# Two hand-made instruction orders replaced, and slabs issued by halves, in a two-layer banded convolution kernel

## The chip, the cores and the metric

The kernel runs on one core of one Trainium2 chip. The metric is the device time of one execution in microseconds (us), as the median of the runs. All arithmetic is in 32-bit floating point; nearly all of it is done by small matmuls on TensorE (PE), with VectorE (DVE), ScalarE (ACT) and GpSimd (POOL) around them, and SyncE (SP) issuing the transfers.

## What is computed

The input x has 512 x 512 positions of 64 channels. Two layers of the same form follow each other, each `x = x + conv(_gn(x))`, where `_gn` normalises groups of two channels over the whole image. The core of one layer, from the reference (the masks are ones, the biases zeros):

```
xn = _ln(x, norm_scale, norm_bias)                       # over the 64 channels
left  = (xn @ Wl + bl) * sigmoid(xn @ Wlg + blg)         # 64 -> 128 channels
right = (xn @ Wr + br) * sigmoid(xn @ Wrg + brg)
out_gate = sigmoid(xn @ Wog + bog)
# _banded_ingoing, w = 4: out[:, i, j] = sum over d = -4..4 of left[:, i+d, i] * right[:, i+d, j]
out = _ln(_banded_ingoing(left, right, 4), out_norm_scale, out_norm_bias) * out_gate
return out @ Wo + bo                                     # 128 -> 64 channels
```

The left part is only needed in the nine diagonals of the band; the right part, the gate and the output are needed at every position.

## The kernel before

**Tiling.** The 512 rows are cut into 9 blocks of 64 rows that step by 56, each block's columns into 4 chunks, and each chunk into 8 units. A layer therefore has 36 chunks and 288 units. The left parts that a block needs lie in SBUF as the tile `A`: 8 slabs, each loaded by two DMAs of 256 KB from `left_of`, one for each half of the partitions. A slab may only be overwritten when the last band of the block that uses it is done.

**Steps.** A unit passes through named steps, each a function `on_...` in `layer`: `load` (two DMAs into `z`), `scale` and `move` (POOL: the group norm), `inner` (DVE: statistics), `centre` and `resc` (POOL), `ztr` (PE: transposes), `keep0/1` (ACT: `ZT`, `zT`), `proj0/1` (PE), `sig0/1` (ACT: `sg`), `right0/1` (DVE: `RO<-banks,sg`). When the eight units of a chunk are there, eight `band` steps (PE: `banks<-RO,A`) and eight `copy` steps (`RO<-banks`) follow. Then, unit by unit: `ost` (DVE: statistics), `gate` (PE: `banks<-ZT,pack`), `gated` (ACT: `ZH<-banks`), `norm0` to `norm7` (ACT or POOL: `on<-RO`), `turn0/1` (PE: `banks<-ident,on`), `tg` (DVE: `ZH<-banks,pack,ZH`), `last` (PE: `bank<-pack,ZH`), `fetch` (two DMAs that load x into `XR`), `end` (DVE: `XR<-bank,XR`), `stp` (two DMAs that store). In layer 1 `sums` (PE: `acc<-XR`) adds up what layer 2's group norm needs; in layer 2 `seed` (PE) starts the output's accumulation. Every four units `sa` (ACT) and `sd0` to `sd13` (DVE) work out the inverse roots (`rs`, `nm`) for the two layer norms.

**What sets the order.** Two tables of words, `FIRST` for layer 1 and `SECOND` for layer 2, are walked once in each period, for `period in range(-4, n_chunks + 5)`. The word `sig1:-13` issues step `sig1` for unit `-13 + 8 * period`. A `!` moves a `norm` from ACT to POOL, a `copy` from ACT to DVE, and a number behind `@` asks for a PSUM bank. The helper `InOrder` (line 504, which is why nearly all rows of the profile carry L504) keeps the order of the program on each engine, so a table is the queue of all five engines; an instruction whose input is late holds up all that stand behind it on its engine.

**Banks.** Three double banks of PSUM (tiles named `banks`) are handed out by `take` and returned by `give`; `ztr`, `proj`, `band`, `gate` and `turn` each take one. PE then waits for the instruction (ACT or DVE) that last read this bank. The sums of layer 1 and the scratch of the inverse roots share one tile, `acc_bank`:

```
acc_bank = psa.tile([P, 512], F32, name="acc")
acc, work = acc_bank[:, : D + 1], [acc_bank[:, P:]]
```

The waits are set by tile, so in layer 1 PE's `sums` and DVE's `sd` steps wait for each other although they use different columns. Layer 2 has a `work` tile of its own and no sums.

**SP.** SP issues every transfer in program order. The semaphores of its DMAs are eight, used in turn, so a DMA also waits for the one eight before it. `slab` issues what stands next in the list `slabs`, to which `on_copy` adds a slab when its last band of a block is copied; where the list is empty the step does nothing, so slabs are loaded at every fourth period, when the row block changes.

Of the kernel before, what the change touches and what calls it, by code (L numbers as in the profile page):

```python
# [38 lines left out]
FIRST = """
end:-14 sd10:-12 inner:-6 sd11:-12 sd9:-12 turn1:-13 proj0:-14@0 proj1:-14@1 sd12:-12 tg:-13  # L40
sig0:-14 norm6:-12 sig1:-14 norm1:-12 resc:-12 resc:-11 norm3:-12! norm4:-12 right0:-14 right1:-14
last:-13 inner:-5 end:-13 inner:-8 band:-12@2 norm5:-12! norm2:-12 norm7:-12! norm0:-12! gate:-11@0
copy:-12 turn1:-12@1 turn0:-12 gated:-11 resc:-10 norm0:-11! ost1:-7 norm7:-11! norm4:-11!
proj1:-13@2 proj0:-13@0 tg:-12 stp:-17 centre:-8 norm2:-11! norm1:-11! centre:-9 load:-1 slab:-56
ost0:-5 sig1:-13 centre:-6 scale:-3 ost1:-5 ost3:-6 ztr:-12@1 norm3:-11 ost2:-7 sums:-16 sums:-15
sums:-17 right1:-13 ost3:-5 last:-12 ztr:-11@2 keep0:-12 keep1:-12 sig0:-13 norm5:-11 norm6:-11
turn0:-11@1 turn1:-11 norm1:-10! ost0:-6 ost3:-8 right0:-13 ost2:-8 end:-12 keep0:-11 keep1:-11
proj1:-12@0 load:0 fetch:-11 norm6:-10! norm0:-10! resc:-9 norm2:-10 scale:-4 tg:-11 proj0:-12@2
ost2:-5 sig1:-12 norm7:-10 right1:-12 ost0:-7 ost2:-6 ost0:-8 ost3:-7 ost1:-6 ost1:-8 gate:-10@1
sig0:-12 norm4:-10 ztr:-10@0 sums:-13 last:-11 norm3:-10 keep1:-10 keep0:-10 right0:-12 end:-11  # L50
gated:-10 sa:-8 sd0:-8 norm5:-10! move:-3 gate:-9@0 turn0:-10@2 gated:-9 norm5:-9! sd1:-8 turn1:-10
proj1:-11@1 tg:-10 sd2:-8 sd3:-8 ost0:-1 sd5:-8 sd4:-8 sig1:-11 load:1 load:2 stp:-12 slab:-112
stp:-14 slab:8 fetch:-10 stp:-13 right1:-11 proj0:-11@0 proj1:-10@2 sums:-14 last:-10 sd6:-8
sig0:-11 norm4:-9 sig1:-10 norm6:-9 norm0:-9! norm3:-9! scale:-1 norm7:-9! norm1:-9! norm2:-9!
right0:-11 ztr:-9@1 sd7:-8 sd8:-8 sd13:-8 right1:-10 turn0:-9@0 turn1:-9 proj0:-10@2 sd10:-8 sd9:-8
move:-4 resc:-8 keep0:-9 keep1:-9 tg:-9 proj1:-9@1 move:-1 resc:-6 sd11:-8 ost3:-4 sd12:-8
proj0:-9@0 sig0:-10 right0:-10 ztr:-8@2 sums:-12 end:-10 sig1:-9 norm1:-8 sig0:-9 right1:-9
right0:-9 last:-9 norm0:-8! scale:-2 norm2:-8 norm6:-8 keep1:-8 band:-6@1 gate:-8@0 load:3 stp:-11
fetch:-9 norm7:-8! norm4:-8! norm3:-8! norm5:-8 keep0:-8 ost0:-3 ost1:-1 turn0:-8@2 turn1:-8 scale:0
centre:-7 norm2:-7! norm6:-7! end:-9 ost2:-3 resc:-7 copy:-6 move:-2 gated:-8 norm5:-7! norm0:-7  # L60
norm7:-7 norm1:-7 gate:-7@1 ost3:-2 norm3:-7 band:-7@0 tg:-8 inner:-4 sums:-10 last:-8 stp:-10
fetch:-8 fetch:-7 scale:1 norm4:-7! gated:-7 copy:-7 ztr:-7@2 ost2:-2 ost0:-2 ost3:-1 ost3:-3
inner:-2 inner:-3 end:-8 gate:-6@1 centre:-5 keep1:-7 gated:-6 keep0:-7 ost1:-3 band:-5@0 copy:-5
turn1:-7@1 turn0:-7 move:1 ost0:-4 proj1:-8@2 proj0:-8@0 tg:-7 norm2:-6 norm0:-6 sig0:-8 ost2:-1
ost1:-4 ost1:-2 ost2:-4 sig1:-8 band:-1@1 norm4:-6! sums:-11 copy:-1 last:-7 move:0 norm3:-6!
resc:-5 norm5:-6! right1:-8 inner:-1 right0:-8 ztr:-6@2 norm6:-6 sa:-4 gate:-5@1 norm1:-6! norm7:-6!
load:4 centre:-3 keep0:-6 keep1:-6 end:-7 sd0:-4 gated:-5 sd1:-4 sd2:-4 slab:-96 band:-3@0 copy:-3
turn0:-6@2 scale:3 scale:2 norm0:-5! turn1:-6 norm6:-5! norm3:-5! proj0:-7@1 proj1:-7@0 sd3:-4
slab:-16 norm2:-5 fetch:-6 sig0:-7 norm1:-5 tg:-6 sd4:-4 sd5:-4 centre:-2 centre:-4 sig1:-7 norm7:-5
slab:40 load:6 fetch:-4 fetch:-5 sd6:-4 band:-8@2 right0:-7 gate:-4@1 sd7:-4 right1:-7 sd8:-4 move:2  # L70
ztr:-5@0 sd13:-4 last:-6 stp:-7 inner:1 copy:-8 norm4:-5 stp:-8 slab:48 slab:0 load:5 move:3
keep0:-5 keep1:-5 norm5:-5 gated:-4 band:-2@2 turn0:-5@0 copy:-2
"""


SECOND = """
gated:-1 slab:-72 load:11 fetch:-1 sd12:0 band:1@2 ost0:5 inner:4 stp:-4 fetch:3 slab:-48 fetch:0
norm5:0 norm3:0 norm0:0 scale:6 copy:1 norm1:0 norm6:0 resc:0 ost1:4 seed:-1 tg:-1 gate:1@0 fetch:1
ztr:0@1 last:-1 band:2@2 keep1:0 keep0:0 gated:1 ost3:7 ost1:7 inner:5 ost2:6 ost1:5 end:-1 resc:1
move:6 norm2:0! norm4:0! turn0:0@1 stp:-1 norm7:0! centre:3 turn1:0 copy:2 norm0:1! seed:0 proj0:0@0  # L80
norm4:1 tg:0 norm3:1! norm5:1! centre:4 scale:11 norm6:1! norm1:1! ztr:1@2 sig0:0 band:6@1 norm7:1
keep1:1 keep0:1 norm2:1 last:0 proj1:0@2 copy:6 ost2:7 inner:7 right0:0 ost1:6 inner:6 load:13
fetch:2 ost0:7 end:0 sa:4 turn1:1@0 turn0:1 seed:1 band:4@1 sd0:4 sig1:0 norm3:2 scale:10 norm2:2!
resc:2 sd1:4 tg:1 sd2:4 right1:0 proj0:1@0 norm4:2 norm6:2 copy:4 sd3:4 gate:2@2 band:5@1 resc:3
norm1:2! norm0:2! move:10 sig0:1 norm7:2 sd5:4 sd4:4 right0:1 move:11 norm5:2 gated:2 turn0:2@0
turn1:2 proj1:1@2 copy:5 scale:9 ztr:2@1 last:1 norm0:3! norm7:3 norm3:3 sig1:1 keep1:2 keep0:2
norm5:3 norm1:3 norm4:3 sd6:4 inner:10 sd7:4 sd8:4 sd13:4 tg:2 norm2:3! scale:13 norm6:3! centre:7
band:7@0 right1:1 end:1 sd10:4 sd11:4 gate:3@2 copy:7! turn1:3@1 turn0:3 sd12:4 gated:3 sd9:4 seed:2
ztr:3@0 last:2 band:3@2 inner:11 tg:3 end:2 keep0:3 norm1:4 move:9 resc:4 norm2:4 centre:5 norm4:4!
norm0:4! norm7:4! seed:3 norm5:4 norm6:4! keep1:3 slab:-16 proj0:2@1 inner:8 inner:9 copy:3 gate:4@0  # L90
centre:6 ost2:8 ost3:11 sig0:2 norm3:4 proj1:2@2 gated:4 load:12 stp:0 sig1:2 right0:2 turn0:4@1
turn1:4 stp:-2 ztr:4@0 slab:32 slab:-8 fetch:4 fetch:5 norm6:5! norm0:5! slab:32 load:16 stp:1
norm7:5 norm2:5! norm4:5! keep1:4 norm3:5 ost2:10 ost1:10 keep0:4 norm5:5! norm1:5 ost2:9 ost3:8
right1:2 last:3 gate:5@2 turn1:5@0 turn0:5 tg:4 resc:7 norm0:6! norm5:6! norm2:6! gated:5 proj0:3@1
end:3 ost1:11 proj1:3@2 norm6:6 sig0:3 resc:5 resc:6 scale:12 norm1:6! centre:8 centre:9 tg:5 sig1:3
norm7:6 norm4:6 seed:4 right0:3 ost0:9 right1:3 proj0:4@0 ost3:10 ost1:8 proj1:4@1 sig0:4 right0:4
sig1:4 norm3:6 ztr:5@2 right1:4 last:4 ztr:6@0 ost0:8 ost1:9 scale:16 slab:40 stp:3 load:15 keep0:5
centre:10 gate:6@1 end:4 keep1:5 ost0:10 ost2:11 ost3:9 keep1:6 keep0:6 gated:6 scale:15 proj0:5@2
turn0:6@0 turn1:6 seed:5 ost0:11 tg:6 proj1:5@1 last:5 ztr:7@0 norm3:7 sig0:5 move:15 ost2:12
fetch:6 sa:8 norm2:7! sig1:5 load:14 load:17 stp:2 slab:48 right0:5 sd0:8 right1:5 end:5 keep0:7  # L100
keep1:7 proj0:6@2 sd1:8 ost3:13 sd2:8 ost0:14 sig0:6 proj1:6@1 sd3:8 sig1:6 proj0:7@0 norm5:7
norm0:7 norm1:7! norm7:7! norm4:7! move:12 right0:6 seed:6 proj1:7@2 sd4:8 right1:6 gate:8@1 sd5:8
ost3:14 sd6:8 sig0:7 norm6:7 sig1:7 right0:7 stp:5 load:18 sd7:8 last:6 right1:7 sd8:8 band:8@0
ost0:12 gated:8 gate:7@2 sd13:8 ost3:12 sd10:8 end:6 sd9:8 move:16 sd11:8 ost2:13 turn1:7@1 turn0:7
move:13 copy:8
"""


# [1214 lines left out]
```

## Time and profile before

| | before |
|---|---|
| median of 3 runs (lowest to highest) | 4062.65 us (4057.47 to 4071.81) |
| profiled execution, its span | 4060.92 us, 4059.1 us |
| PE busy | 3652.7 us, 90% of the span |
| weight loads of PE (PEld) busy | 3167.1 us, 78% |
| DVE busy | 3592.6 us, 89% |
| ACT busy | 3222.3 us, 79% |
| POOL busy | 3562.2 us, 88% |
| granted clock, mean | 0.992 |
| DMA engines, mean busy | 50% by q1 (all of SP's transfers, 579.92 MB), 1.3% by q8 (instructions, 12.26 MB) |

The span is one run through the whole program. Its first 336.5 us are the statistics of the input, the weights and the filling of the pipeline of layer 1; from there to 2107.9 us layer 1 runs in periods of eight units, each with about 1378 PE instructions, and after the change of layers layer 2 does so from 2299.1 to 3993.1 us. In both of these stretches the granted clock is 1.00. Four engines are busy for 79 to 90% of the span, so the busy shares alone don't tell which one sets the time; the stretches of single periods do.

### The profile page before, as it was taken

Reading aid. Unit: us, or ns where it says so; the run is one execution under the profiler, and the core shown is the slowest. Engines: PE = TensorE matmul, PEld = TensorE weight load, DVE = VectorE, ACT = ScalarE, POOL = GpSimd, SP = SyncE. Lnnn points to the kernel's source line nnn. Section 1 sums busy time; section 2 is a strip of 40 time slices with the busy share of each in tenths; the row PEclk is TensorE's granted clock in tenths of the full one; section 3 lists DMA queues with packets and bytes.
Section 4 is the critical chain, followed back from the end, with each engine's and each line's share of the span. In section 5 each row is a group of like instructions: output and inputs, shape, how many; then the busy total and the mean of one; then the engine's idle time right before and its main releaser. Section 6 shows DMA issues by size and latency. Waiting matters only on the chain. (4 is left out here: it accounts for less than half of the span.)

```text
span 4059.1 us, 222567 instructions
## 1 busy us (share of the span) xinstructions
PE 3652.7 (90%) x94986; PEld 3167.1 (78%) x94986; DVE 3592.6 (89%) x9915; ACT 3222.3 (79%) x6120; POOL 3562.2 (88%) x4818
## 2 busy tenths in 40 slices
...
GB/s 397 334 130 95 155 117 154 120 160 116 157 119 154 116 146 123 147 128 151 133 100 120 128 155 128 154 132 158 130 160 122 159 126 157 127 160 124 165 111 103
DMA packets 562867, 595.72 MB, mean 147 GB/s; under 512 B 134742, under 2 KB 398966, under 8 KB 559572
## 3 DMA queue, kind: packets, MB, share of 16 engines
q1 hardware_dynamic: 559364, 579.92, 50.0%
q8 instruction: 748, 12.26, 1.3%
...
## 5 line engine op out<-in xcount | busy, mean ns | idle before, releaser
L504 POOL TENSOR_SCALAR on<-RO,rs,nm 128x128 f32<-128x128 f32 x2376 | 1050.4, 454 | 220.8 <-PE banks L504 174.7
L504 ACT ACTIVATE on<-RO,nm,rs 128x128 f32<-128x128 f32 x2232 | 1029.0, 500 | 24.0 <-PE banks L504 15.5
L504 PE MATMUL banks<-pack,ZT 64*128 64x128 f32 x9216 | 980.0, 282 | 35.0 <-DVE acc L504 14.9
L504 PE MATMUL banks<-pack,zT 64*128 64x128 f32 x9216 | 935.1, 273 | 0.6 <-issue 0.5
L504 ACT ACTIVATE sg<-banks 128x512 f32<-128x512 f32 x1170 | 691.7, 594 | 244.2 <-PE banks L504 215.9
L504 DVE BATCH_NORM_STATS2 sto<-RO 128x6 f32<-128x256 f32 x2304 | 859.6, 413 | 18.0 <-ACT RO L504 18.0
L504 DVE TENSOR_TENSOR RO<-banks,sg 128x512 f32<-128x512 f32 x1152 | 785.1, 683 | 93.8 <-ACT sg L504 74.9
L504 PEld LDWEIGHTS banks<-pack,ZT 64*128 64x128 f32 x9216 | 758.7, 189 | 82.2 <-PE banks L504 18.6
L504 DVE SCALAR_TENSOR_TENSOR ZH<-banks,pack,ZH 128x896 f32<-128x896 f32 (+1 forms) x576 | 667.6, 1159 | 134.4 <-PE banks L504 81.1
L504 PEld LDWEIGHTS banks<-RO,A 64*64 64x64 f32 x36864 | 614.2, 135 | 211.3 <-ACT ZH L504 45.4
L504 PE MATMUL banks<-RO,A 64*64 64x64 f32 x36864 | 698.5, 222 | 63.4 <-issue 26.2
L504 PEld LDWEIGHTS banks<-pack,zT 64*128 64x128 f32 x9216 | 746.9, 189 | 0.6 <-issue 0.6
L504 POOL TENSOR_TENSOR z<-z,rs 128x512 f32<-128x512 f32 x586 | 611.4, 1054 | 93.3 <-DVE rs L504 67.2
L504 PE MATMUL bank<-pack,ZH 128*64 128x64 f32 x18432 | 658.0, 224 | 25.1 <-DVE ZH L504 12.0
L504 POOL TENSOR_TENSOR z<-z,ga 128x512 f32<-128x512 f32 x556 | 649.9, 1172 | 32.4 <-DVE ga L425 18.0
L504 PEld LDWEIGHTS bank<-pack,ZH 128*64 128x64 f32 x18432 | 588.1, 138 | 85.0 <-issue 35.3
L504 POOL TENSOR_TENSOR z<-z,gb 128x512 f32<-128x512 f32 x556 | 645.2, 1171 | 3.1
L504 ACT COPY RO<-banks 128x1024 f32<-128x1024 f32 x540 | 547.0, 1013 | 106.2 <-PE banks L504 94.5
L504 POOL TENSOR_TENSOR z<-z,sti 128x512 f32<-128x512 f32 x586 | 621.3, 1069 | 5.5 <-DVE sti L504 5.5
L504 ACT ACTIVATE ZH<-banks 128x896 f32<-128x896 f32 (+1 forms) x576 | 535.5, 930 | 88.6 <-PE banks L504 45.7
L504 PE MATMUL banks<-ZT,pack 64*128 64x448 f32 (+1 forms) x2304 | 585.0, 575 | 2.0 <-issue 1.7
L504 DVE BATCH_NORM_STATS2 sti<-z 128x6 f32<-128x128 f32 x2344 | 506.6, 281 | 30.0 <-POOL z L504 29.6
...
## 6 DMA issues: line engine op xcount, KB each, us to landing
...
A<-left_of SPq DMA_DIRECT2D x288, 256.0 KB
...
```

The costliest lines, as they stand in the source:

```text
L504: return lambda *a, **k: tc.keep_in_program_order(f(*a, **k))
```

## The change

The two tables are replaced as a whole. No word of the new ones names a bank, and `take` hands out the bank that has been free longest, where it handed out the lowest-numbered free one. A `slab` word issues one half of a slab (one DMA) instead of both, and each new table has 16 such words instead of 8; the number and the sizes of the DMAs stay. In `FIRST` three of 35 `norm` steps per period go from POOL to ACT; in `SECOND` 31 of them stay on POOL, and the one `copy` on DVE goes to ACT. The lag between a unit's `proj` and its `end` stays at two periods, the tables' first and last words move by some units. All else that is computed, and every instruction of PE, is the same.

```diff
 FIRST = """
...
-stp:-14 slab:8 fetch:-10 stp:-13 right1:-11 proj0:-11@0 proj1:-10@2 sums:-14 last:-10 sd6:-8
...
+ost0:9 ost1:8 norm0:5 sums:0 sums:2 sig1:3 ost3:10 ost2:9 ost3:8
...
+norm2:5! norm3:5! sums:-1 sums:1 ost2:11 ost0:11 right1:3 last:4 slab:0
...
 SECOND = """
...
     def take(b: str) -> tuple:
 
         free = [n for n in range(3) if given[n] is not None]
-        n = int(b) if b else free[0]
+        n = int(b) if b else -1
         if loose[0] or n not in free:
             n = min(free, key=lambda m: given[m])
         given[n] = None
...
-    def take_left(n: int, h: int):
-
-        held[h] = n
-        for e in range(2):
-            en.sync.dma_start(
-                A[e * S : (e + 1) * S, h].rearrange("p h i t -> p (h i t)"),
-                strided(
-                    left_of, left_at(n) + h * HA // 2 * span,
-                    (H // 2 * span, S), (1, HA // 2 * span),
-                ),
-            )
+    def take_left(n: int, h: int, e: int):
+
+        if e:
+            held[h] = n
+        en.sync.dma_start(
+            A[e * S : (e + 1) * S, h].rearrange("p h i t -> p (h i t)"),
+            strided(
+                left_of, left_at(n) + h * HA // 2 * span,
+                (H // 2 * span, S), (1, HA // 2 * span),
+            ),
+        )
...
         for h in range(H // HA):
-            posts.setdefault(1, []).append(lambda h=h: slabs.append((0, h)))
+            posts.setdefault(1, []).append(lambda h=h: slabs.extend((0, h, e) for e in range(2)))
...
                 if (c + 1) % per == 0 and c + 1 < n_chunks:
-                    slabs.append(((c + 1) // per, h))
+                    slabs.extend(((c + 1) // per, h, e) for e in range(2))
```

How the tables move instructions is seen in the order of each engine; a row is one instruction or several alike, and the line is that of the helper (L504 before, L522 after).

**PE, layer 1, about the middle of a steady period.** Before, the calls `acc<-XR` (sums) stand singly, each ahead of a `last`; these two lie 17 rows apart:

```order
L504 MATMUL banks<-pack,zT 128x2x64 x2
L504 MATMUL acc<-XR_1091 64x65 x8
L504 MATMUL bank<-pack,ZH_1093 64x64 x16
L504 MATMUL banks<-ident,z 128x64 x8
L504 MATMUL banks<-ident,on 128x64 x16
...
L504 MATMUL banks<-ident,z 128x64 x8
L504 MATMUL acc<-XR_1087 64x65 x8
L504 MATMUL bank<-pack,ZH_1094 64x64 x16
L504 MATMUL banks<-RO,A 64x64 x32
```

Of the new table the same place, with the rows ahead of it:

```order
L522 MATMUL banks<-pack,zT 128x2x64 x2
L522 MATMUL banks<-ident,on 128x64 x16
L522 MATMUL banks<-ident,z 128x64 x8
L522 MATMUL acc<-XR_1091 64x65 x8
L522 MATMUL acc<-XR_1087 64x65 x8
L522 MATMUL acc<-XR_1090 64x65 x8
L522 MATMUL acc<-XR_1092 64x65 x8
L522 MATMUL bank<-pack,ZH_1093 64x64 x16
```

Four sums now stand behind one another, ahead of one `last`.

**DVE, layer 1, the inverse roots around those sums.** The rows with `acc`, `rsqrt_t`, `rsqrt_u`, `rs` are the `sd` steps; `RO<-banks,sg` is `right`, `ZH` is `tg`. Before:

```order
L504 TENSOR_TENSOR acc<-acc,rsqrt_u 128x64
L504 TENSOR_TENSOR rsqrt_t<-acc,rsqrt_u 128x64
L504 TENSOR_TENSOR RO<-banks,sg 128x64x8
L504 SCALAR_TENSOR_TENSOR rsqrt_u<-rsqrt_t,acc 128x64
L504 TENSOR_TENSOR RO<-banks,sg 128x64x8
L504 SCALAR_TENSOR_TENSOR acc<-rsqrt_u,acc 128x64
```

And of the change, the run of `sd` steps that is the last one ahead of the four sums:

```order
L522 TENSOR_TENSOR rsqrt_u<-acc,var 128x64
L522 TENSOR_TENSOR rsqrt_t<-acc,rsqrt_u 128x64
L522 TENSOR_TENSOR XR_1092<-bank,XR_1092 120x4x128
L522 TENSOR_TENSOR acc<-acc,rsqrt_u 128x64
L522 SCALAR_TENSOR_TENSOR ZH_1093<-banks,pack,ZH_1093 128x16x56
L522 SCALAR_TENSOR_TENSOR rsqrt_u<-rsqrt_t,acc 128x64
```

The steps themselves are the same, and `right` and `end` stand between them as before. What has moved is where PE's sums lie: the words `sums:0`, `sums:2`, `sums:-1`, `sums:1` come after `sd12:4`, the last word of one run, and before `sa:8`, which opens the next; `sums:3` stands right before `sa:8` and `sums:-2` right before `sa:4`. Before, `sums:-14` stood between `sd4:-8` and `sd6:-8`.

**SP, layer 1, where the row block changes.** `A<-left_of` is a slab's half, `z<-in_x_dram` a load, `XR<-in_x_dram` a fetch, `mid_x<-XR` a store. Before:

```order
L504 DMA z<-in_x_dram 64x512 x2
L504 DMA A<-left_of 64x1024 x4
L504 DMA XR_1087<-in_x_dram 60x4x128 x2
L504 DMA A<-left_of 64x1024 x2
L504 DMA z<-in_x_dram 64x512 x2
L504 DMA XR_1089<-in_x_dram 60x4x128 x2
L504 DMA XR_1088<-in_x_dram 60x4x128 x2
L504 DMA mid_x<-XR_1092 60x4x128 x2
L504 DMA mid_x<-XR_1091 60x4x128 x2
L504 DMA A<-left_of 64x1024 x4
```

And of the change:

```order
L522 DMA A<-left_of 64x1024
L522 DMA z<-in_x_dram 64x512 x2
L522 DMA A<-left_of 64x1024
L522 DMA XR_1092<-in_x_dram 60x4x128 x2
L522 DMA A<-left_of 64x1024
L522 DMA mid_x<-XR_1090 60x4x128 x2
L522 DMA A<-left_of 64x1024 x3
L522 DMA z<-in_x_dram 64x512 x4
L522 DMA A<-left_of 64x1024
```

Halves that stood four and two together now stand mostly singly between other transfers. In `SECOND` they stand less far apart: runs of three, one, one, three and two follow each other with loads and fetches between them.

## Rows read from the trace of the kernel before

**Rows 1.** Stretches (from:to): length; busy us of PE, PEld, DVE, ACT, POOL; PEclk; DMA.

```profile
1374.90:1426.10 51.20, 50.41 (x1378) 44.22 (x1376) 45.48 (x124) 44.10 (x84) 49.56 (x68) 1.00 0.47 122
3093.40:3142.20 48.80, 48.13 (x1259) 42.08 (x1257) 45.63 (x126) 44.32 (x87) 47.72 (x64) 1.00 0.44 125
...
336.50:2107.90 1771.40, 1723.06 (x46694) 1505.17 (x46684) 1544.72 (x4201) 1502.34 (x2818) 1659.02 (x2256) 1.00 0.51 134
2299.10:3993.10 1694.00, 1647.30 (x42697) 1436.88 (x42696) 1552.81 (x4226) 1511.59 (x2922) 1595.95 (x2119) 1.00 0.49 140
```

**Rows 2.** DVE's `tg`, layer 1, then layer 2: count, ns min/median/max, first and last start.

```profile
L504 DVE SCALAR_TENSOR_TENSOR ZH<-banks,pack,ZH x273: 1122/1149/1220, 336.5 to 2107.9; 128x896 f32<-128x896 f32 x112, 128x960 f32<-128x960 f32 x25
...
L504 DVE SCALAR_TENSOR_TENSOR ZH<-banks,pack,ZH x273: 1124/1149/1220, 2299.1 to 3993.1; 128x896 f32<-128x896 f32 x112, 128x960 f32<-128x960 f32 x25
```

**Rows 3.** Waits of PE, 336.5 to 2107.9 (layer 1): us in all, times, longest.

```profile
PE banks L504 <- DVE acc L504: 14.9, 34, 0.5
PE banks L504 <- issue: 13.3, 15, 2.1
PE banks L504 <- DVE RO L504: 10.8, 32, 0.3
PE bank L504 <- DVE XR L504: 5.3, 5, 1.6
PE bank L504 <- issue: 2.9, 3, 1.4
```

**Rows 4.** Waits of PE, 2299.1 to 3993.1 (layer 2).

```profile
PE banks L504 <- ACT ZH L504: 17.6, 33, 0.6
PE banks L504 <- issue: 16.7, 25, 1.6
PE bank L504 <- DVE XR L504: 5.0, 7, 1.6
PE bank L504 <- issue: 3.4, 4, 1.2
```

**Rows 5.** Timeline, 1416 to 1419: start, us, instruction, [idle before <- releaser].

```profile
1416.08 0.22 DVE L504 SCALAR_TENSOR_TENSOR rsqrt_u<-rsqrt_t,acc 128x64 f32<-128x64 f32 x1 [0.42 <-PE acc L504]
...
1416.90 0.46 PE L504 MATMUL banks<-ident,z 64*128 64x64 f32 x8
...
1417.20 0.66 PE L504 MATMUL banks<-ident,on 64*128 64x64 f32 x16
...
1418.31 0.49 PE L504 MATMUL banks<-pack,ZT 64*128 64x128 f32 x4 [0.45 <-DVE acc L504]
...
1418.56 1.04 POOL L504 TENSOR_TENSOR z<-z,rs 128x512 f32<-128x512 f32 x1 [0.80 <-DVE rs L504]
```

**Rows 6.** The costliest groups of the page: busy us, mean ns of one, idle before.

```profile
L504 POOL TENSOR_SCALAR on<-RO,rs,nm 128x128 f32<-128x128 f32 x2376 | 1050.4, 454 | 220.8 <-PE banks L504 174.7
L504 ACT ACTIVATE on<-RO,nm,rs 128x128 f32<-128x128 f32 x2232 | 1029.0, 500 | 24.0 <-PE banks L504 15.5
```

**Rows 7.** Timeline, 689 to 698, in a block change of layer 1.

```profile
689.66 1.03 SPq L504 DMA_DIRECT2D XR<-in_x_dram  x2
...
696.47 0.69 DVE L504 TENSOR_TENSOR XR<-bank,XR 120x512 f32<-120x512 f32 x1 [2.16 <-DMA XR<-in_x_dram]
```

**Rows 8.** Timeline, 645 to 656, in the same block change.

```profile
645.65 2.77 SPq L504 DMA_DIRECT2D A<-left_of  x4
...
655.13 0.94 PE L504 MATMUL banks<-RO,A 64*64 64x64 f32 x44 [1.60 <-issue]
```

**Rows 9.** Timeline, 1395 to 1400: two projections, a `last`, a band and its copy.

```profile
1395.26 0.44 PE L504 MATMUL banks<-pack,ZT 64*128 64x128 f32 x4
...
1397.19 1.15 PE L504 MATMUL bank<-pack,ZH 128*64 128x64 f32 x32
...
1398.69 1.19 PE L504 MATMUL banks<-RO,A 64*64 64x64 f32 x64 [0.35 <-DVE RO L504]
...
1399.95 1.01 ACT L504 COPY RO<-banks 128x1024 f32<-128x1024 f32 x1 [0.87 <-PE banks L504]
```

More of the change, by code (lines that the diff above doesn't have):

```diff
@@ L39 @@
 FIRST = """
[L40 to L51, printed above, removed]
@@ L58 @@
[L58 to L69, printed above, removed]
@@ L70 @@
-slab:40 load:6 fetch:-4 fetch:-5 sd6:-4 band:-8@2 right0:-7 gate:-4@1 sd7:-4 right1:-7 sd8:-4 move:2
-ztr:-5@0 sd13:-4 last:-6 stp:-7 inner:1 copy:-8 norm4:-5 stp:-8 slab:48 slab:0 load:5 move:3
-keep0:-5 keep1:-5 norm5:-5 gated:-4 band:-2@2 turn0:-5@0 copy:-2
+band:1 scale:8 move:6 norm1:1! norm6:1! scale:10 norm0:1 gated:1 sums:-3
+last:0 norm2:1 copy:1 ztr:1 gate:2 norm3:1 centre:3 band:3 keep1:1
+keep0:1 norm4:1! norm7:1 scale:9 norm5:1! gated:2 turn1:1 turn0:1 inner:4
+copy:3 ost1:5 centre:7 move:9 proj0:0 ost3:7 ost0:4 ost2:4 end:0
@@ new lines @@
+ost1:6 ost0:7 fetch:2 proj1:0 sig0:0 tg:1 band:7 inner:6 ost0:5
+right0:0 sig1:0 sums:-2 last:1 ztr:2 ost2:6 slab:0 load:11 slab:0
+fetch:1 slab:0 stp:-1 norm4:2 copy:7 sa:4 right1:0 keep0:2 keep1:2
+norm1:2 sd0:4 sd1:4 move:8 norm5:2! norm3:2! norm6:2! centre:4 norm7:2!
+norm2:2! gate:3 gated:3 norm0:2! slab:0 slab:0 slab:0 band:5 turn1:2
+sd2:4 turn0:2 proj1:1 copy:5 norm6:3 norm1:3 inner:9 sig1:1 move:10
+scale:11 proj0:1 end:1 sd3:4 sd4:4 sd5:4 load:12 load:13 slab:0
+tg:2 right1:1 norm3:3 sig0:1 band:0 proj0:2 right0:1 sd6:4 inner:10
@@ new lines @@
+copy:0 sd7:4 sd8:4 norm0:3! resc:3 move:11 norm2:3! norm5:3 sig0:2
+ztr:3 right0:2 sd13:4 sd10:4 keep0:3 keep1:3 gate:4 sd9:4 inner:8
+sd11:4 centre:5 scale:12 norm4:3! norm7:3 last:2 end:2 sd12:4 band:6
+turn0:3 gated:4 copy:6 turn1:3 proj1:2 tg:3 norm3:4 sig1:2 norm7:4
+norm0:4 proj0:3 sig0:3 scale:13 resc:4 norm5:4! norm2:4! norm1:4 resc:5
+norm6:4! centre:6 resc:7 right1:2 band:4 stp:-3 copy:4 norm4:4 last:3
+ztr:4 keep1:4 right0:3 inner:11 keep0:4 gate:5 gated:5 proj1:3 slab:0
+fetch:3 slab:0 slab:0 stp:0 turn0:4 turn1:4 ztr:5 end:3 ost2:10
@@ new lines @@
+ost0:9 ost1:8 norm0:5 sums:0 sums:2 sig1:3 ost3:10 ost2:9 ost3:8
+tg:4 norm1:5! norm5:5! stp:-2 keep1:5 norm7:5 keep0:5 norm6:5 move:12
+norm2:5! norm3:5! sums:-1 sums:1 ost2:11 ost0:11 right1:3 last:4 slab:0
+slab:0 slab:0 fetch:4 turn1:5 stp:2 stp:1 ost1:10 ost3:9 ost1:11
+end:4 load:14 slab:0 fetch:5 norm4:5 resc:6 turn0:5 gate:6 tg:5
+norm7:6! norm2:6 norm4:6 proj0:4 centre:9 norm6:6! norm3:6 gated:6 ost2:8
+ost1:9 load:15 fetch:6 slab:0 stp:3 ost0:8 centre:10 fetch:7 ost3:11
+ost0:10 proj1:4 ztr:6 sig0:4 sig1:4 sums:3 last:5 right0:4 slab:0
```

86 lines of the change are left out of this document (52 added, 34 removed).

## The prediction, as made before the result was known

> **What bounds the kernel now.** I read the stretches first, because the shares of the whole span mix two layers and their ends. From the first to the last of the 273 `tg` steps of a layer there are 272 / 8 = 34 periods [rows 2]; layer 1 takes 1771.4 us for them, layer 2 1694.0 [rows 1], so 52.1 and 49.8 us each. The undisturbed periods are shorter, 51.20 and 48.80 [rows 1]: 34 of these make 1740.8 and 1659.2, and the excess over them is 30.6 and 34.8 us.
>
> In an undisturbed period of layer 1 PE is busy for 50.41 of 51.20 us, POOL for 49.56, DVE for 45.48, ACT for 44.10; in layer 2 PE for 48.13 of 48.80, POOL for 47.72 [rows 1]. The clock is 1.00 in both, so nothing is lost there. PE is the bound, with POOL 0.4 to 0.9 us behind it: a table can win no more than the 0.79 and 0.67 us that PE is idle, unless it also shortens the calls, and in layer 2 POOL allows at most 1.08.
>
> What ends PE's idle time comes from its waits. In layer 1 two waits return in nearly every period, on `DVE acc` (14.9 us in 34 times) and on `DVE RO` (10.8 in 32); beside them stand gaps that no wait explains ("issue", 13.3 + 2.9) and late `XR` (5.3) [rows 3]. In layer 2 one returns, on `ACT ZH` (17.6 in 33), with gaps of 16.7 + 3.4 and late `XR` of 5.0 [rows 4].
>
> The timeline shows where the first comes from. At 1416.08 DVE's `rsqrt_u`, a step of the inverse roots, has waited 0.42 us for PE's sums, which write other columns of the same tile; DVE's `right` steps stand behind it, so PE's projection at 1418.31 waits 0.45 for its bank, and POOL's `resc` at 1418.56 has waited 0.80 for `rs` [rows 5]. One false dependence stalls three engines.
>
> **The change part by part.**
>
> *Sums and inverse roots.* In the new order every sum of layer 1 lies between two runs of `sd` steps and none within one. DVE no longer has to stop for PE inside a run, which removes the 14.9 us. The price is that four sums stand together: they wait for the last `end` and for the end of the run, and `last` stands behind them on PE. The tile makes `sa` wait for the sums too, but these are ahead of it in the table, with other work between. I see no longer wait there than the 0.42 of [rows 5], and an ACT wait is covered: ACT is busy for 44.10 of 51.20.
>
> *Other places of layer 1's order.* The `DVE RO` wait goes if `right` stands earlier ahead of the first band. Laying the rows of the new order behind each other with the durations of the trace, I find no input of PE late by more than 0.05 us at a period of 50.4. Together the two are worth 14.9 + 10.8, **−26 us**; the lower bound is nothing, the upper 34 x 0.79 = 27.
>
> *Norms.* Three go from POOL to ACT: POOL falls to 49.56 − 3 x 0.454 = 48.2, ACT rises to 44.10 + 3 x 0.500 = 45.6 [rows 1, 6]. Neither bounds; the cover is ACT's 7.1 us idle. That takes POOL away as the next bound: without it a PE period of 50.4 would leave POOL 0.9 of slack.
>
> *Layer 2.* Its inverse roots have a tile of their own, so nothing is freed but the places where inputs are late. The wait on `ACT ZH` is worth 17.6 us. POOL's 47.72, the same 31 norms, allows 34 x 1.08 = 36.7 at most, if calls that now stretch because their inputs trickle in are also shortened. I take the middle, **−27 us** (a period of 48.0); the lower bound is nothing again. The `copy` that goes from DVE to ACT adds 1.0 us [rows 9] to ACT's 44.32: covered.
>
> *Half slabs.* The same DMAs, spread. Before, four halves go out at 645.65 in 2.77 us, two more by 651.6, and a band at 655.13 breaks off after 20 matmuls and goes on 1.60 us later with no wait named [rows 8]. In the same block change a fetch issued at 689.66 isn't there for the `end` at 696.47, which waits 2.16 us [rows 7]. Late `XR` costs PE 5.3 + 5.0 us. In layer 1 halves now stand singly between loads and fetches; in layer 2 three at a time, still ahead of fetches. I take 5 + 3, **−8** (bounds 0 and −10.3). The unexplained gaps are 16.2 + 20.1 = 36.3 us; that they come of PE's instructions arriving late behind slabs is likely from [rows 8], but the trace names no cause. I take **−3**, since the same bytes pass in the same block change; bounds 0 and −36.3.
>
> The Trainium skill, "Runtime: NRT & Kernel Launch", Instruction fetch mechanics, says that crossing an instruction block's boundary is mostly hidden; by that rule the gaps are not fetches and this term is 0. "DMA: Bandwidth & Descriptors", Queues, rings and completion order, says that an engine alternates between queues after each packet; so a slab would hold a fetch of instructions up by packets only, and spreading slabs would change little. The trace neither confirms nor refutes them: the gaps come where slabs are issued, but no row shows a fetch. They keep the term small and rival C unlikely.
>
> *Banks.* No instruction is added; which bank a step takes only decides whose release it waits for. Longest-free is never later than lowest-numbered by the order of releases: 0.
>
> *What the tighter order costs.* With PE never idle by plan, small delays that a slack of 0.8 us took up now reach PE. The nearest rows price a place where PE just misses its input at 10.8 / 32 = 0.34 and 14.9 / 34 = 0.44 [rows 3]. I take a third of one in each of 68 periods, 0.12 us, **+8** (bounds 0 and 68 x 0.44 = +30).
>
> *Ends of the layers.* The lag of two periods stays; a table that begins elsewhere moves the first and last units by some us either way: 0, bounds ±10.
>
> Sum: −26 − 27 − 8 − 3 + 8 = −56 against the profiled execution's 4060.92, so 4004.9. The median of the runs is 1.7 above it: **4006.6 us**.
>
> **The rivals.**
>
> *A, the waits only move.* The old tables were laid out by the same kind of plan and yet have these waits, so new ones may leave as many. For it: in layer 2 nothing is freed by knowledge of the tile. Against it: in layer 1 the waits have one visible cause, and it is gone. Periods stay at 51.2 and 48.8, transfers bring −11: 4049.9 + 1.7 = 4051.6.
>
> *B, slower: banks that ACT frees, in the first half of layer 1's period.* There the new order puts most bands, each with a copy on ACT, and I count six PE calls whose bank is freed by a `copy` or `gated` just as PE comes to it. One of them: a band, a projection, a `ztr`, then a `gate` on the bank that the band's copy frees. From the band's start the copy starts 1.26 us later and takes 1.01 [rows 9], so it ends at 2.27. PE's band (1.19, at most), projection (two take 1397.19 − 1395.26 = 1.93, so 0.96 [rows 9]) and `ztr` (0.30 from 1416.90 to 1417.20 [rows 5]) end at 2.45. The margin is 0.18, and ACT must not be behind. If each of the six is late by one ACT `norm`, 0.5 us [rows 6], the period is 50.4 + 3.0 = 53.4 and layer 1 loses 34 x 2.2 = 75 us; with −27 − 11 that gives 4060.9 + 37 + 1.7 = 4100. It decides from 0.38 us a place: 34 x (6 x 0.38 − 0.79) is 50, 12 more than the other terms give. Against it: ACT has 5 us of slack per period, and a delay at one place relieves the next.
>
> *C, the block changes go smoothly too.* Of the excess of 65 us, 46.6 is idle time (36.3 in gaps, 10.3 by `XR`) and 20 is longer PE calls: 1723.06 − 34 x 50.41 = 9 and 1647.30 − 34 x 48.13 = 11 [rows 1]. If all of it goes, 33 + 2 + 20 more are saved: 3952. For it: single halves in layer 1. Against it: runs of three remain in layer 2.
>
> **How the numbers follow.** The forecast has 0.60, with a range of its own of 3975 to 4040 (bounds of layer 2's term and of the gaps on one side, of the new waits on the other); A 0.17, B 0.09, C 0.14. 0.3%, about what a measurement of this kernel can tell, is 12 us: 4050.5 and 4074.8. Faster is the forecast and C, less 0.02, and nearly half of A: 0.80; the same the rest of A and 0.02: 0.11; slower 0.09. The range reaches from within C to past A, 3965 to 4058; it leaves out half of C and all of B, 0.16, and some tails.
>
> **What would show it.** Right: undisturbed periods of 50.4 to 50.6 and 47.9 to 48.2 us; `DVE rsqrt_u <- PE acc` and `PE <- DVE acc` gone in layer 1; POOL about 48.2 there; fewer waits on `XR`. Wrong: PE waiting on `ACT RO` or `ACT ZH` at banks in layer 1 (B), the old lengths with other releasers (A), no gaps without a wait at block changes (C). What would make it wrong on either side most easily is a block change: sixteen slab words can hold up SP's loads and fetches where eight did not, each waiting for its band in turn.

## The result, and the profile after

The changed kernel takes 3994.95 us (median of 4 runs, 3991.41 to 4000.14), before it takes 4067.23 (4 runs, 4057.47 to 4072.9); the ratio is 0.9826, with a 95% interval of 0.9801 to 0.9851. It is 72 us faster by the medians; the two profiled executions, 3997.06 and 4060.92 us, lie 63.9 apart, and it is these that the stretches below divide up. In experiment 6 one of five executions took 7412.04 us, and its ratio leaves this one out.

The stretches from the first to the last full period of the two layers, and the change of layers between them, columns as in [rows 1]:

```profile
1357.10:1407.30 50.20, 50.20 (x1388) 44.30 (x1383) 45.16 (x125) 45.19 (x87) 48.16 (x65) 1.00 0.48 121
...
2999.00:3047.30 48.30, 48.30 (x1262) 42.02 (x1261) 44.99 (x125) 45.35 (x88) 47.97 (x64) 1.00 0.40 123
325.00:2075.90 1750.90, 1725.11 (x46730) 1514.45 (x46728) 1536.65 (x4194) 1539.83 (x2922) 1613.75 (x2154) 1.00 0.51 136
2266.50:3928.00 1661.50, 1645.01 (x42705) 1430.52 (x42705) 1530.98 (x4191) 1538.83 (x2956) 1596.39 (x2118) 1.00 0.50 143
2075.90:2266.50 190.60, 132.95 (x3038) 111.04 (x3038) 154.45 (x446) 105.31 (x193) 122.75 (x146) 0.89 0.46 123
```

In the two quiet periods shown PE is now busy from end to end: 50.20 of 50.20 us in layer 1 and 48.30 of 48.30 in layer 2, with POOL at 48.16 and 47.97. The one of layer 1 is among its shortest. Counted from a `tg` to the eighth behind it, the median of the 26 periods without a change of the row block went from 51.21 to 50.75 us in layer 1 and from 49.11 to 48.30 in layer 2, and the eight with one went in sum from 434.5 to 428.9 and from 413.3 to 401.8. PE's idle time in all 34 fell from 48.3 to 25.8 us and from 46.7 to 16.5; its busy time moved by +2.1 and −2.3. The 34 periods of layer 1 went from 1771.4 to 1750.9 us (−20.5), those of layer 2 from 1694.0 to 1661.5 (−32.5) [rows 1]. Layer 1's first `tg` starts at 325.0 in place of 336.5 [rows 2]: −11.5 before any steady period. What is left of the span, the change of layers (190.6, before 2299.1 − 2107.9 = 191.2 [rows 2]) and the end (67.3, before 66.0), moved by less than 1.5 us.

PE's waits, layer 1 and then layer 2, in us, times, longest, as in [rows 3] and [rows 4]:

```profile
PE banks L522 <- issue: 15.3, 29, 1.1
PE bank L522 <- issue: 3.9, 4, 1.6
PE banks L522 <- ACT RO L522: 2.2, 4, 1.0
PE banks L522 <- DVE rsqrt_u L522: 1.3, 1, 1.3
...
PE acc L522 <- DMA XR<-in_x_dram: 0.4, 1, 0.4
```

```profile
PE banks L522 <- issue: 12.8, 17, 1.2
PE banks L522 <- POOL on L522: 1.4, 2, 1.1
PE bank L522 <- issue: 1.3, 4, 0.6
```

The three recurring waits (`DVE acc` 14.9, `DVE RO` 10.8, `ACT ZH` 17.6) are gone, and so are, but for 0.4 us, PE's waits on late `XR` (10.3). What remains in the main are the gaps that no semaphore ends, 33.3 us (19.2 + 14.1), where there were 36.3.

### The profile page after: what moved, and what is told of

It reads as the page before. It is cut to its first block, busy times and chain, and to the rows that moved or that the text cites. A ratio compares the mean times of both kernels' runs of the same rounds, so it can differ in the third digit from the quotient of the medians.

```text
span 3995.3 us, 222970 instructions
## 1 busy us (share of the span) xinstructions
PE 3656.0 (92%) x94986; PEld 3174.2 (79%) x94986; DVE 3563.5 (89%) x9879; ACT 3290.3 (82%) x6264; POOL 3518.4 (88%) x4710
## 4 chain that ended last, share of the span: by engine, by line
PE 82%; DVE 6%; DMA 5%; POOL 3%; issue 2%; SPq 1%; ACT 1%; DVEq 0%; POOLq 0%; ACTq 0%
PE banks L522 63%; PE bank L522 15%; PE acc L522 4%; POOL z L522 2%; DVE gn_st L522 2%; DVE RO L522 1%; DMA raw<-in_L_conv_Wr_dram 1%; DVE sto L522 1%; SPq L522 1%; DMA z<-mid_x 1%; DVE ZH L522 1%; DVE z L522 1%; POOL on L522 0%; DVE XR L522 0%; DMA raw<-in_L_conv_Wl_dram 0%
## 5 line engine op out<-in xcount | busy, mean ns | idle before, releaser
L522 POOL TENSOR_SCALAR on<-RO,rs,nm 128x128 f32<-128x128 f32 x2268 | 1012.0, 457 | 257.1 <-PE banks L522 225.6
L522 ACT ACTIVATE on<-RO,nm,rs 128x128 f32<-128x128 f32 x2340 | 1085.4, 503 | 59.2 <-PE banks L522 31.8
L522 PE MATMUL banks<-pack,ZT 64*128 64x128 f32 x9216 | 958.4, 283 | 19.9 <-DVE RO L522 13.0
L522 PE MATMUL banks<-pack,zT 64*128 64x128 f32 x9216 | 915.4, 274 | 3.2 <-issue 3.1
L522 DVE TENSOR_TENSOR RO<-banks,sg 128x512 f32<-128x512 f32 x1152 | 786.5, 686 | 139.2 <-ACT sg L522 106.9
L522 DVE BATCH_NORM_STATS2 sto<-RO 128x6 f32<-128x256 f32 x2304 | 840.4, 412 | 12.0 <-ACT RO L522 11.9
L522 ACT ACTIVATE sg<-banks 128x512 f32<-128x512 f32 x1170 | 697.6, 596 | 165.4 <-PE banks L522 139.4
L522 PEld LDWEIGHTS banks<-pack,ZT 64*128 64x128 f32 x9216 | 733.4, 189 | 103.4 <-issue 38.7
L522 DVE SCALAR_TENSOR_TENSOR ZH<-banks,pack,ZH 128x896 f32<-128x896 f32 (+1 forms) x576 | 666.6, 1157 | 147.1 <-PE banks L522 92.7
L522 PEld LDWEIGHTS banks<-RO,A 64*64 64x64 f32 x36864 | 613.2, 135 | 172.5 <-issue 53.0
L522 PEld LDWEIGHTS banks<-pack,zT 64*128 64x128 f32 x9216 | 723.3, 190 | 4.4 <-issue 4.2
L522 PE MATMUL banks<-RO,A 64*64 64x64 f32 x36864 | 694.3, 221 | 32.1 <-issue 23.2
L522 POOL TENSOR_TENSOR z<-z,ga 128x512 f32<-128x512 f32 x556 | 653.1, 1175 | 40.8 <-DMA z<-mid_x 22.7
L522 PE MATMUL bank<-pack,ZH 128*64 128x64 f32 x18432 | 660.4, 224 | 17.3 <-DVE ZH L522 8.5
L522 ACT COPY RO<-banks 128x1024 f32<-128x1024 f32 x576 | 579.2, 1012 | 105.1 <-PE banks L522 98.8
L522 POOL TENSOR_TENSOR z<-z,gb 128x512 f32<-128x512 f32 x556 | 651.4, 1175 | 3.4
L522 PEld LDWEIGHTS bank<-pack,ZH 128*64 128x64 f32 x18432 | 588.4, 138 | 73.7 <-issue 31.9
L522 POOL TENSOR_TENSOR z<-z,rs 128x512 f32<-128x512 f32 x586 | 620.6, 1063 | 27.7 <-DVE rs L522 23.3
L522 POOL TENSOR_TENSOR z<-z,sti 128x512 f32<-128x512 f32 x586 | 625.1, 1070 | 5.0 <-DVE sti L522 5.0
L522 PE MATMUL banks<-ZT,pack 64*128 64x448 f32 (+1 forms) x2304 | 580.5, 576 | 3.2 <-ACT RO L522 2.2
L522 ACT ACTIVATE ZH<-banks 128x896 f32<-128x896 f32 (+1 forms) x576 | 534.8, 929 | 50.4 <-PE banks L522 47.5
L522 DVE BATCH_NORM_STATS2 sti<-z 128x6 f32<-128x128 f32 x2344 | 514.3, 282 | 11.7 <-POOL z L522 11.2
```

What stands on the lines that cost most here:

```text
L522: return lambda *a, **k: tc.keep_in_program_order(f(*a, **k))
```

## The experiments

Ratios below are against runs of the kernel before on the same chip, since chips differ by some 0.4%.

**1 and 2. One table at a time.** The new table in one layer, the old one with its whole slabs and named banks in the other. Beside the table, the edit of experiment 1 (`stats` is true in layer 1; experiment 2 has `2 if stats else 1`):

```diff
-            if slabs:
-                take_left(*slabs.pop(0))
+            for _ in range(1 if stats else 2):
+                if slabs:
+                    take_left(*slabs.pop(0))
```

> The new table in layer 1 alone, the old one in layer 2 (whole slabs and its named banks there). If the two layers' gains add up as the stretches of the two traces read (start of layer 1 earlier by 11.5 us, its 34 periods shorter by 20.5, layer 2 shorter by 32.5), this gains about 32 us: some 4035 us beside 4067 of before. If the gain needs both tables together (the change of layers, or transfers that one layer leaves behind for the other), it differs from 32 by more than 10 us.

> The new table in layer 2 alone, the old one in layer 1. By the stretches of the two traces the 34 periods of layer 2 get shorter by 32.5 us and the ends by about nothing: some 4034 us beside 4067 of before, and a start of layer 1 at 336 as before. If the earlier start of layer 1 has nothing to do with its table, it is seen here too (325).

Measured: 4029.83 us for the new table in layer 1 (ratio 0.9903, 0.9880 to 0.9926) and 4041.45 in layer 2 (0.9926, 0.9904 to 0.9948): −0.97% and −0.74%, together −1.71%, where the whole change gives −1.74%. The gains add up within the intervals of about 0.23 points each, so no part of that size lies between the layers. Layer 1's `tg` starts at 326.5 with its new table and at 336.2 with its old one, so the earlier start belongs to that layer's part of the change.

**3 and 4. Sums and inverse roots in separate tiles.** PSUM has no bank left, so the scratch of layer 1's inverse roots went to SBUF.

```diff
-    acc_bank = psa.tile([P, 512], F32, name="acc")
-    acc, work = acc_bank[:, : D + 1], [acc_bank[:, P:]]
+    acc = psa.tile([P, 512], F32, name="acc")[:, : D + 1]
+    work = [keep.tile([P, 8 * NB], F32, name="work")]
```

> The kernel before with the scratch of layer 1's inverse roots in a tile of its own in SBUF, so that sums and inverse roots no longer share a tile; order unchanged. If the shared tile is what ends PE's recurring 0.44 us wait, the waits on acc go, a quiet period of layer 1 falls from 51.2 to 50.4 to 50.8 and the kernel gains 15 to 26 us (4041 to 4052). If the order itself puts these steps too late, another releaser stands in the same place and the time stays within 8 us of 4067.

> The same separation of the two tiles in the changed kernel. If the new order has taken the shared tile out of the way, nothing is left to gain: 3995 us within 6. If the four sums in a row still wait for the inverse roots, or these for them, it gains 10 us or more.

Measured: 4383.42 us (ratio 1.0778, 1.0746 to 1.0809) and 4232.16 (1.0390, 1.0352 to 1.0428). Neither theory had this. The groups of DVE in layer 1 of the first of the two (busy us, mean ns):

```profile
L504 DVE TENSOR_TENSOR rsqrt_t<-work,rsqrt_u 128x64 f32<-128x64 f32 x135 | 146.8, 1087 | 2.3
L504 DVE TENSOR_TENSOR work<-work,pack 128x32 f32<-128x32 f32 x67 | 116.9, 1744 | 0.2 <-ACT work L504 0.2
L504 DVE TENSOR_TENSOR rsqrt_u<-work,var 128x64 f32<-128x64 f32 x135 | 64.5, 478 | 3.5
```

and the first two of these in the kernel before, by the same kind of view, where `acc` is in PSUM:

```profile
L504 DVE TENSOR_TENSOR rsqrt_t<-acc,rsqrt_u 128x64 f32<-128x64 f32 (+1 forms) x136 | 30.0, 221 | 3.5
L504 DVE TENSOR_TENSOR acc<-acc,pack 128x32 f32<-128x32 f32 x68 | 13.2, 194 | 4.7 <-ACT acc L504 1.3
```

A quiet period of experiment 3, columns as in [rows 1]:

```profile
1266.30:1327.60 61.30, 53.84 (x1378) 46.82 (x1376) 55.22 (x124) 44.15 (x84) 49.56 (x68) 0.94 0.35 98
```

The same instruction takes 1087 ns on average with both inputs in SBUF and 221 with one in PSUM. DVE is busy for 55.22 us in place of 45.48, and the granted clock is 0.94 where it was 1.00. The experiments thus say nothing on the shared tile: they exchanged one cost for a larger one.

**5. One sum moved out of the run, in the kernel before.**

```diff
-ztr:-10@0 sums:-13 last:-11
+ztr:-10@0 sums:-13 sums:-14 last:-11
...
-proj1:-10@2 sums:-14 last:-10 sd6:-8
+proj1:-10@2 last:-10 sd6:-8
```

> The kernel before with one word of FIRST moved: sums:-14 goes from between sd4 and sd6 of a run of inverse roots to right behind sums:-13, ahead of the run (once a period; nothing else changes). If the shared tile with this one sum inside a run makes the recurring wait, PE's 14.9 us on acc and DVE's 0.42 a period on PE acc go, a quiet period of layer 1 falls from 51.2 to about 50.8, and the kernel gains 10 to 20 us. If the wait only moves to the next late input, periods stay at 51.1 to 51.2 and the time within 5 us of before.

Measured: 4072.03 us against 4073.88 (ratio 1.0003, 0.9991 to 1.0016): no change. PE's waits in its layer 1:

```profile
PE banks L504 <- DVE RO L504: 19.1, 65, 0.4
PE banks L504 <- issue: 10.9, 16, 1.7
PE bank L504 <- DVE XR L504: 6.8, 5, 2.0
```

PE's groups that wait for DVE there (busy us, mean ns, idle before):

```profile
L504 PE MATMUL banks<-pack,ZT 64*128 64x128 f32 x4352 | 440.1, 279 | 8.9 <-DVE RO L504 8.0 <-issue 0.8
L504 PE MATMUL banks<-RO,A 64*64 64x64 f32 x17372 | 331.3, 222 | 18.1 <-DVE RO L504 11.1 <-issue 6.1
```

and one quiet period of it, columns as in [rows 1]:

```profile
1381.30:1432.40 51.10, 50.51 (x1378) 44.18 (x1376) 45.55 (x125) 44.18 (x84) 49.56 (x68) 1.00 0.48 121
```

The wait on `acc` is gone from PE and from DVE, as expected. But `DVE RO` now comes 65 times where it came 32 times [rows 3], the period is 51.10 where it was 51.20, and PE's idle time of 0.59 is 0.2 less, of which 0.1 went into longer calls. At the projection 8.0 of the 14.9 us are left: its inputs are `pack` and `ZT`, so what it now waits for is a bank that `right` has yet to read. The band's wait was 10.8 and is 11.1; the tile had no part in it. The shared tile was the last of the projection's late inputs, and another stood close behind it.

**6 and 7. One sum put into a run, in the changed kernel.**

```diff
-ost0:10 proj1:4 ztr:6 sig0:4 sig1:4 sums:3 last:5 right0:4 slab:0
+ost0:10 proj1:4 ztr:6 sig0:4 sig1:4 last:5 right0:4 slab:0
...
-sd4:8 end:5 sd5:8
+sd4:8 end:5 sd5:8 sums:3
```

> The reverse in the changed kernel: sums:3 goes from just ahead of sa:8 into the run behind it, between sd5:8 and sd6:8. If one sum inside a run is what costs, DVE waits for PE acc about 0.4 us a period again, and the kernel loses 5 to 20 us against 3995. If the new order has enough slack behind these steps, it loses less than 4.

> The changed kernel with sums:3 moved into the run of inverse roots once more, for an undisturbed trace: 15 to 22 us more than the changed kernel, as its timed runs showed. If the shared tile is the reason, DVE waits for PE acc, or PE for DVE acc, once a period with 0.3 us or more, and PE stands behind it; if it is only that a late sum delays its store and the fetch into the same buffer, waits on XR appear instead.

Measured: 4014.26 us (ratio 0.9852, 0.9830 to 0.9875) and, on another chip, 4002.89 (0.9868, 0.9853 to 0.9882): 22 and 11 us more than experiments 8 and 12 on the same two chips (3991.97 and 3991.42), and by the ratios 11 and 17 us more than the changed kernel (0.9826), whose interval the first one overlaps. The wait came back on DVE, in layer 1 of the second run:

```profile
DVE rsqrt_u L522 <- PE acc L522: 16.5, 34, 0.6
```

34 times 0.49 us; the changed kernel has none. Waits on `XR` didn't appear. The 34 periods of this run, columns as in [rows 1]:

```profile
326.00:2085.30 1759.30, 1739.82 (x46730) 1519.24 (x46728) 1534.52 (x4193) 1537.67 (x2922) 1618.84 (x2154) 1.00 0.51 135
```

They are 8.4 us longer than the changed kernel's, whose new table took 1748.7 to 1754.3 us in three other traces (experiments 1, 8 and 12). PE shows no wait by name; its busy time is 14.7 us more and its idle time 6.3 less. So a sum in a run does cost in the new order, and DVE waits for it; that PE's calls are longer because of this wait is argued, as no row links the two.

**8. Whole slabs in the new tables.** Both halves at every second slab word.

```diff
-            if slabs:
-                take_left(*slabs.pop(0))
+            words[0] += 1
+            for _ in range(2 - words[0] % 2 * 2):
+                if slabs:
+                    take_left(*slabs.pop(0))
```

> The changed kernel with whole slabs: both halves issued at every second slab word, none at the first. My terms for the spreading of halves were 8 us by late XR and 3 by gaps without a wait; if they hold, this loses about 10 us (4000 to 4008) and waits on XR come back. If the better place of the fetches in the new tables made the XR waits go, it stays within 4 us of 3995 and no XR wait returns.

Measured: 3991.97 us (ratio 0.9803, 0.9781 to 0.9824), no slower than with halves. DVE has no wait on a fetch into `XR`, where the kernel before has 34.1 us of them in all (21.9 in layer 1, 12.2 in layer 2), and PE's gaps without a wait come to 29.0 us, no more than with halves. The halves gained nothing. What is left to have removed the `XR` waits is the new tables, in which the fetches stand elsewhere; the fetches alone were not moved.

**9. The lowest-numbered free bank in the new tables.**

```diff
-        n = int(b) if b else -1
+        n = int(b) if b else free[0]
```

> The changed kernel with the lowest-numbered free bank in place of the one free longest; the order of every engine is the same. I gave the bank rule 0. If the tables are made for the rule, PE's calls in the first half of layer 1's period, which come just behind the ACT instruction that frees a bank, wait for the release that came last: waits of PE on ACT RO and ACT ZH of 0.2 us or more at several places in each period, and 20 us or more lost. If banks are mostly alone in being free, it stays within 5 us of 3995.

Measured: 5030.56 us (ratio 1.2356, 1.2326 to 1.2385), 1036 more than the changed kernel by the medians, with the same order on every engine. One period of layer 1, columns as in [rows 1], and PE's waits in it:

```profile
1208.30:1275.40 67.10, 54.63 (x1376) 45.65 (x1376) 46.06 (x125) 46.11 (x87) 48.14 (x65) 0.96 0.34 90
```

```profile
PE banks L522 <- ACT ZH L522: 4.1, 4, 1.6
PE banks L522 <- DVE ZH L522: 2.1, 3, 1.3
PE banks L522 <- ACT zT L522: 1.6, 1, 1.6
PE banks L522 <- ACT ZT L522: 1.2, 1, 1.2
PE banks L522 <- ACT RO L522: 1.2, 1, 1.2
PE banks L522 <- DVE RO L522: 1.1, 2, 0.6
```

`ACT ZH`, `DVE ZH` and `ACT RO` are the steps `gated`, `tg` and `copy`, which read out a bank and write nothing that the waiting calls read: PE was handed a bank that was not yet read out. The other three may be banks or inputs. The granted clock is 0.96 there, and PE is busy 4.4 us longer than in the changed kernel's period, so not all of the 16.9 us more is waiting.

**10. The bank free longest in the old tables.** All `@` words struck out of both old tables, the new rule in `take`.

```diff
-proj0:-14@0 proj1:-14@1
+proj0:-14 proj1:-14
...
-        n = int(b) if b else free[0]
+        n = int(b) if b else -1
```

> The kernel before with all its named banks struck out and the bank free longest handed out: the bank rule of the change alone. If names and rule come to the same, the time is within 5 us of before. If a table and its banks belong together, PE waits at banks several times a period and it loses 30 us or more.

Measured: 4102.61 us against 4056.78 (ratio 1.0113, 1.0096 to 1.0130). Its layer 1, by `tg` as in [rows 2], and its layer 2, as in [rows 1]:

```profile
L504 DVE SCALAR_TENSOR_TENSOR ZH<-banks,pack,ZH x273: 1124/1148/1222, 327.0 to 2089.8; 128x896 f32<-128x896 f32 x112, 128x960 f32<-128x960 f32 x25
```

```profile
2283.80:4031.90 1748.10, 1654.33 (x42697) 1430.14 (x42696) 1553.74 (x4225) 1515.85 (x2922) 1600.58 (x2119) 1.00 0.48 135
```

PE's longest waits in its layer 1, and then in its layer 2:

```profile
PE banks L504 <- DVE acc L504: 15.0, 34, 0.5
```

```profile
PE banks L504 <- ACT ZT L504: 45.0, 68, 0.7
```

Layer 1 starts at 327.0 in place of 336.5 and its 34 periods take 1762.8 us, 8.6 less than before; two more traces with the old table and its names (experiments 2 and 5), one execution each, have 1777.3 and 1775.8. The wait on `DVE RO` [rows 3] is gone without a step of the order moved, and the one on `DVE acc` stays. Layer 2's periods take 1748.1, 54.1 more, with the wait on `ACT ZT`. So the rule alone gives 9.5 of the 11.5 us at the start of layer 1, and 8.6 us or more in its periods. From 260 us to this start PE waits 7.7 us on `DVE RO`, where it was 14.0 before; that the named banks collide there because an unfilled pipeline leaves steps out, I only argue. The old order of layer 2 needs its names.

**11. An eighth of each slab's bytes.**

```diff
+        m = HA // 2 * span if n == 0 else HA // 2 * span // 8
...
-            A[e * S : (e + 1) * S, h].rearrange("p h i t -> p (h i t)"),
+            A[e * S : (e + 1) * S, h].rearrange("p h i t -> p (h i t)")[:, :m],
...
-                (H // 2 * span, S), (1, HA // 2 * span),
+                (H // 2 * span, S), (1, m),
```

> The changed kernel with an eighth of each slab's bytes from the second block on (512 bytes of the 4096 in each row; the bands then use what the first block left): the same number of DMAs, waits and words. If the gaps of PE without a wait (19.2 us in layer 1, 14.1 in layer 2 of the changed kernel) come of the slabs' bytes, they fall below 10 us in all, and the time to 3960 to 3975. If they come of PE's own stream of instructions or of the number of transfers, 25 us or more of them stay and the time is above 3985.

Measured: 3949.38 us (ratio 0.9737, 0.9722 to 0.9751), 42 less than experiment 12 on the same chip. PE's gaps without a wait, layer 1 and layer 2:

```profile
PE banks L522 <- issue: 1.9, 6, 0.6
...
PE bank L522 <- issue: 0.2, 1, 0.2
```

```profile
PE banks L522 <- issue: 4.6, 8, 1.2
PE bank L522 <- issue: 0.4, 2, 0.2
```

A period with a block change, columns as in [rows 1]:

```profile
628.20:678.40 50.20, 50.20 (x1386) 44.29 (x1380) 45.11 (x125) 45.23 (x87) 48.27 (x65) 1.00 0.46 129
```

7.1 us are left of 33.3 (33.6 in experiment 12), which is 26 of the 42 us; 14.8 more are shorter PE calls, by PE's busy time in both layers beside experiment 12. The period with a block change takes 50.20 us like a quiet one. The number of transfers, words and waits is the same, so the gaps come of the slabs' bytes. The kernel leaves out seven eighths of these bytes, so it is a measure of their cost and no faster version.

**12. Three norms back on POOL.**

```diff
-norm7:3 ... norm0:5 ... norm2:8
+norm7:3! ... norm0:5! ... norm2:8!
```

> The changed kernel with three norms of layer 1's table back on POOL (norm7:3, norm0:5 and norm2:8): POOL rises by 3 x 0.457 to about 49.5 us a period, still below PE's 50.2. If POOL's slack of 0.7 us is enough, it stays within 5 us of 3995. If POOL is late with norms wherever it is nearly full, PE waits on POOL on at its turns and it loses 10 us or more.

Measured: 3991.42 us (ratio 0.9841, 0.9827 to 0.9856): the same time within the intervals. A quiet period of layer 1:

```profile
1356.70:1407.30 50.60, 50.20 (x1372) 44.34 (x1364) 45.25 (x125) 43.46 (x83) 49.65 (x68) 1.00 0.48 123
```

POOL is busy for 49.65 of 50.60 us, and PE's waits on POOL's `on` come to 0.5 us in all 34. The move of the three norms gained nothing that can be measured.

## Why the prediction was right, step by step

The sum was −56 us against the profiled execution; 63.9 were measured, and the median of 3994.95 lies 11.7 below the forecast. Its largest statement held: in both layers PE's recurring waits go, and quiet periods become PE's busy time almost from end to end (50.75 and 48.30 us by the median, where 50.4 to 50.6 and 47.9 to 48.2 stood as signs). By the terms of the sum the two spans differ by −25.7 (layer 1), −22.9 (layer 2), −10.3 (late `XR`), −3.0 (gaps), +8.9 (new waits) and −10.8 (ends), −63.8 in all. Several steps behind the terms did not hold, and part of the agreement is luck: the ends, priced at 0, gave what layer 2 fell short by, and more.

- **Sums and inverse roots, and other places of layer 1 (−26).** The size was right: the waits worth 25.7 us are gone. What failed is the worth of the cause, in "which removes the 14.9 us": experiment 5 took the dependence out of the old order and got nothing, since the projection then waited 8.0 of these 14.9 us for a bank that `right` reads, and the 34 periods got no shorter. The cause told for the second wait failed too, in "goes if `right` stands earlier": experiment 10 removes it by the bank rule alone, with `right` where it was. In the new order one sum put back costs 11 to 22 us (experiments 6 and 7). The old order with the bank rule and the moved sum together was not run, so whether the rest of the new order was needed for this term is open. The sum also missed a new wait at this place: DVE now waits for `sa` in every period, 0.88 us on average, where the kernel before had 1.3 us in 7 times. The sums are not its reason, since ACT waits only 0.3 us in all for them, and it cost PE next to nothing (1.3 us on `rsqrt_u`).

```profile
DVE acc L522 <- ACT acc L522: 29.9, 34, 2.0
```

- **Layer 2 (−27).** Measured for its 34 periods: −32.5. Of this, −5.0 is late `XR` and −6.0 gaps, which the sum has under the half slabs, and +1.4 new waits; the term itself is −22.9: the wait on `ACT ZH` (−17.6), shorter calls (−2.3) and other short idle times (−3.0). It was taken somewhat too large: the quiet period fell to 48.30 in the row shown, where 48.0 was forecast, and POOL, at 47.97 of 48.30, now leaves little. No experiment took the order of this layer apart, so which moved step removed the wait isn't shown.
- **Half slabs (−8 and −3).** Both sizes were close (−10.3 and −3.0), but experiment 8 shows that the halves had no part in either, so that the sizes fit is luck. The late `XR` went with the new tables, in which the fetches stand elsewhere. The gaps are from the slabs' bytes (experiment 11), which nothing in the change reduces; the term was small for the reason given.
- **Banks (0).** This is the step that failed most. By the trace of experiment 10, the rule alone is worth 9.5 us at the start of layer 1 and 8.6 in its periods, while it costs 54.1 in the old order of layer 2; and the new tables can't do without it: experiment 9 loses 1036 us. "Which bank a step takes only decides whose release it waits for" is true, but these releases had a price.
- **Ends of the layers (0, bounds ±10).** Measured −10.8, just outside the bounds, nearly all at the start of layer 1, 9.5 of it by the bank rule (experiment 10).
- **New waits (+8).** In layer 1 5.5 us of new idle time, by name or short, and 2.0 of longer calls; in layer 2 1.4 on POOL. The size was right, 8.9. Of the 20.5 us of layer 1: −25.7 (recurring waits) −5.3 (`XR`) +3.0 (gaps, 16.2 to 19.2) +7.5 (these).
- **Norms (0).** Right, by experiment 12; the words that this "takes POOL away as the next bound" were not needed.
- **Rival B** did not come: PE waits on ACT at banks of layer 1 for 2.4 us in 34 periods (2.2 on `RO`, 0.2 on `ZH`). With banks taken in another order they do come: in the one period shown of experiment 9, five waits on `ACT ZH` and `ACT RO` with 5.3 us. That they are the six places of the prediction isn't shown. **Rival C** would need fewer bytes at a block change; experiment 11 shows it at −42 us with an eighth of them.

Two rules of the Trainium skill were set against these gaps. "Runtime: NRT & Kernel Launch", Instruction fetch mechanics, has the crossing of an instruction block mostly hidden; "DMA: Bandwidth & Descriptors", Queues, rings and completion order, has an engine switch between queues after a packet. No view lists a single fetch, but the trace holds every packet of queue q8 (instructions). In the 34 + 34 periods of the kernel before these are 704 of 16 KB, one for 254 matmuls and weight loads of PE. All 47 gaps that no semaphore ends are over 1.20 to 1.76 us after the end of such a packet; the time from 1.2 to 1.8 us behind a packet is 12% of these stretches. In the changed kernel it is 50 of 54 gaps, with 32.1 of the 33.3 us, and in experiment 11 still 15 of 17. So these gaps are PE waiting for its own instructions, and more slab bytes make more packets come too late for PE. The first rule agrees as far as it goes, since 657 of the 704 packets pass without such a gap; what failed is the step from it, "by that rule the gaps are not fetches". How a slab's transfer holds a packet up, and so whether the second rule has a part, no run shows.

No variant that moves all bytes beat the changed kernel by more than the intervals: whole slabs (0.9803) and three norms back on POOL (0.9841) lie within the interval of 0.9826.
